# First inputs of three graph pairs in buffers of later work, weights in long runs, a re-tuned static plan, and a last layer norm by row halves

## Chip, core and metric

The kernel runs on one core of a Trainium2 chip. All times are device microseconds of one execution. A profile of one execution shows where the time goes inside it; its "span" runs from the first to the last instruction.

## What is computed

64 graphs of 256 nodes with 256 features go through two layers. Everything is in fp32.

```python
# layer 0: two graph attention steps, layer norm, feed-forward, layer norm
h = gat(x, adj, W1, a1); h = gat(h, adj, W2, a2)      # softmax(where(adj > 0, leaky_relu(e), NEG)) @ (h @ W)
h = layernorm(x + h);    h = layernorm(h + relu(h @ w_ff1 + b) @ w_ff2 + b)        # 256 -> 1024 -> 256
# layer 1: attention with 8 heads, whose weights are sorted by relation (adj == r), then the same feed-forward shape
q, k = h @ Wq, h @ Wk
out  = sum over r of (softmax(q k^T / sqrt(32)) * (adj == r)) @ (h @ Wv[r])
x = layernorm(h + out @ Wo);  out = layernorm(x + gelu(x @ W1 + b1) @ W2 + b2)
```

## The kernel before

**Tiling.** Two graphs make a pair, and 32 pairs go through `whole_way(pair)`: `gat_layers`, `feed_forward` (layer 0), `attention`, `feed_forward` (layer 1), then two stores of 256 KB. Every product is fp32 and is issued by `by_strips`, a helper at L166: four matmuls, each on 32 columns of the array. Nearly all products therefore stand under L166 in the profile, and tiles tell them apart. The products of the feed-forward and of q, k and v are done with seven block products in place of eight (the classes `Second` and `Blocks`, and `by_seven`), which needs sums of weight blocks, made once at the start (`block_sums` L446, `last_sums` L440).

**Order.** The order of instructions on every engine is fixed before the kernel runs. `run` is a list scheduler: it keeps a modelled clock per engine (`clock`, set from `START`), lets up to six pairs be under way, and asks each time which step can begin first. Steps of TensorE are chosen by a degree per kind, work of the other engines by a rank per kind. A step counts as ready when its events have happened in the model: a piece of work ends after its modelled duration plus a `lag` of 0.2 us, and TensorE prefers a step that has been ready for at least `slack` us. The table `CHANGES` resets ranks, degrees, slack and step orders at fixed model times, most of them 90 us apart, which is about one pair. `keep_order` then pins the emitted order. Each engine runs its own instructions strictly in that order, so a wait of the first one holds up all behind it.

**The first loads.** For pairs 0 and 1, `load(pair, at)` issues xT (the features, transposed), adjT (the adjacency) and x at once, and the plan is told when they land: 6.5 us and 18.0 us. For weights it is told 8, 15, 30 and 37 us. All go through the DMA queue of SP. xT of either pair goes to the one buffer `input`, so the xT of pair 1 can only be fetched once pair 0 has been read. Weights for the block products are fetched block by block: four loads of 256 KB for each of the four feed-forward matrices, eight of 64 KB for q and k, four of 128 KB for v. The later pairs are loaded by `load(pair)` with the plan's own events; their adjT and xT share `input`.

**What waits on a load.** `small_adj` (L390, ScalarE) turns adjT into bytes, `largest` (L394, VectorE) looks for empty columns. In `addends` the exponentials (L582 to L584) and a spreading over all partitions follow; in `gat_weights` VectorE makes attention weights (L630, L632) and ScalarE scales the rows (L639). L650 takes products out of the PSUM banks. L1170 and the lines near it fold biases through the weights, once.

**Layer norm.** `means` (L719) or `add_rows` gives the means of two rows-of-128, `layernorm` adds squares (L733, ScalarE), a root on GpSimd (L738, L739), and centring and scaling (L744, L747, VectorE). It works on the two row chunks of one graph. The result is turned by `transposed`: VectorE turns 32x32 blocks into `yb` (L780), SP stores them to DRAM (`home`) and gathers them back as `yT` (L785, L791); ScalarE copies `yT` into `yTa` for the attention (L973). For a few pairs at both ends (`hurried`) TensorE turns them instead (L811).

Of the kernel before, what the change touches and what calls it, by code (L numbers as in the profile page):

```python
# [10 lines left out]
F32 = mybir.dt.float32  # L11
# [7 lines left out]
P = 128  # L19
# [7 lines left out]
HURRIED = 2  # L27
SEVEN = (0, 2)
SHAPES = ("rows",)
NORMED = ()  # L30
CHANGES = (
    (27.0, ("all", "slack", 0.2), ("rank", "means", 0)),
    (117.0, ("rank", "means", 1)),
    (207.0, ("all", "qkv", ("a1", "b1", "b2", "a2", "a6", "a5", "b6", "a7", "a4", "b5", "b7", "a3", "b4", "s0", "b3", "s1")),
     ("rank", "adj", 1), ("rank", "normalise", 2), ("rank", "exp", -1)),
    (297.0, ("degree", "fill", 1), ("all", "groups", (([0], []), ([1], []), ([], [2]), ([], [3]), ([2], []), ([3], []))),
     ("degree", "first", -1), ("all", "slack", 0.3)),
    (387.0, ("degree", "fill", 2.5), ("all", "slack", 0.8), ("rank", "mask", 1.5), ("rank", "turn", 2),
     ("all", "first", ("a1", "b1", "a6", "a2", "b2", "b6", "a5", "a7", "b7", "a4", "b5", "b4", "a3"))),
    (477.0, ("all", "slack", 0.1)),  # L40
    (657.0, ("rank", "qk", 2), ("rank", "adj", 0), ("rank", "act", 0.5), ("rank", "last", 0.5)),
    (1197.0, ("rank", "invert", 1.5), ("rank", "adj", -1), ("rank", "exps", -0.5),
     ("all", "first", ("a1", "b1", "a2", "a6", "b2", "b6", "a5", "a7", "b7", "a4", "b5", "b4", "a3")),
     ("rank", "normalise", 0), ("degree", "rows", 2)),
    (1287.0, ("rank", "turn", 1)),
    (1377.0, ("all", "groups", (([0], []), ([1], []), ([], [2]), ([], [3]), ([2], []), ([3], []))), ("rank", "divide", 1.5),
     ("rank", "copies", -2), ("all", "flight", 5)),
    (1467.0, ("all", "first", ("a1", "b1", "a2", "a6", "b2", "b6", "a5", "a7", "b7", "b5", "a4", "b4", "a3")),
     ("rank", "addends", 0.5)),
    (1557.0, ("rank", "copies", 1), ("rank", "qk", -2)),  # L50
    (1827.0, ("rank", "copies", -2)),
    (1917.0, ("rank", "v", 1)),
    (2007.0, ("rank", "rows", 1.5), ("rank", "squares", -0.5), ("rank", "copies", 0)),
    (2367.0, ("rank", "last", 1), ("rank", "adj", -0.5), ("degree", "attention", 0)),
    (2547.0, ("rank", "divide", 1), ("rank", "mask", 3)),
    (2637.0, ("degree", "first", 2.5)),
    (2727.0, ("rank", "last", 3), ("rank", "second", 0.5)),
    (2817.0, ("all", "first", ("a1", "b1", "a2", "a6", "b2", "b6", "a5", "a7", "b7", "b5", "a4", "b4", "a3")),
     ("rank", "second", -0.5), ("rank", "rows", -2)),
# [6 lines left out]
        "normalise": -1, "copies": -2, "seeds": -2, "act": -1, "last": -1, "sums": -0.5, "qk": 1, "v": 1.5, "exp": 3, "mask": 0, "halves": 0, "invert": 3,  # L66
# [5 lines left out]
START = {"tensor": 8.5, "vector": 8.0, "scalar": 4.0, "gpsimd": 0.0, "sync": 32.0}  # L72
# [3 lines left out]
def two_layers(ctx: ExitStack, tc: tile.TileContext, t: dict, out: bass.AP, flag: bass.AP):  # L76
# [98 lines left out]
    nc.sync.dma_start(right[:, :, :D], t["L0_gnn_W2"].rearrange("(c p) m -> p c m", p=P))  # L175
    nc.scalar.dma_start(a2, bass.AP(tensor=t["L0_gnn_a2"].tensor, offset=t["L0_gnn_a2"].offset, ap=[[0, P], [1, 2 * D]]))
    nc.sync.dma_start(w1T, t["L0_gnn_W1T"].rearrange("(c p) m -> p c m", p=P))
# [7 lines left out]
    for columns in (slice(0, D), slice(D, D + 4)):  # L185
        for m in range(KC):
            for c in range(KC):
                by_strips(both[m][:, columns], lhsT=w1T[:, c, m * P:(m + 1) * P], rhs=right[:, c, columns],
                          start=c == 0 and columns.start == 0, stop=c == KC - 1, skip_group_check=True)
    for m in range(KC):  # L190
        nc.vector.tensor_copy(w12[:, m], both[m][:, :D + 4])
# [15 lines left out]
    free = {name: [0.0] * n for name, n in (("bank", 8 - KEPT), ("kept", KEPT), ("a", HQ), ("m", HQ), ("h", HQ), ("yb", 1), ("yT", 2), ("yTa", 1),  # L207
# [15 lines left out]
    def put(engine, us, emit, *events, rank=1, lag=0.2, kb=0, function=None, needs=None, frees=(), event=None, behind=None):  # L223
# [46 lines left out]
    def took(us):  # L270

        clock["tensor"] += us
        return at_time(clock["tensor"] + 0.2)
# [14 lines left out]
    def run(besides, ways):  # L288
# [12 lines left out]
        while True:  # L301
# [42 lines left out]
            else:  # L344
# [6 lines left out]
                clock[engine] += piece["us"]  # L351
# [10 lines left out]

    def of_graph(b):
        return slice(2 * b, 2 * b + 2)


    def load(pair, at=None):
# [4 lines left out]
        def adjT():  # L372
            if at is not None:
                to["adjT"] = work.tile([P, 2, 2, 2 * D], F32, name="v")[:, pair].bitcast(I32).rearrange(
                    "p b (c n) -> p (b c) n", c=2)
            else:
                to["adjT"] = io.tile([P, 4, N], I32, name="input")
            nc.sync.dma_start(to["adjT"], t["adjT"][rows].rearrange("b (c p) n -> p (b c) n", p=P))

        def xT():  # L380
            to["xT"] = io.tile([P, KC, 512], F32, name="input")
            nc.sync.dma_start(to["xT"], t["xT"][pair].rearrange("(c p) b n -> p c (b n)", p=P))
# [20 lines left out]
        if at is None:  # L403
# [4 lines left out]
        for emit in (xT, adjT, x):  # L408
            emit()
        return to, [at_time(at), in_bytes(at_time(at)), at_time(at)]  # L410

    def first_weights(name, wide=None):

        w = t[name]
        rows = w.shape[1] // 2
        s = const.tile([P, 7, rows], F32, name="w_" + name)
        for c, at in ((0, (0, 2)), (1, (1, 6))):
            for half, n in enumerate(at):  # L420
                nc.sync.dma_start(s[:, n], w[c * P:(c + 1) * P, half * rows:(half + 1) * rows])
        return s
# [8 lines left out]
    def last_weights(name):  # L431

        s = const.tile([P, 7, NF // 2, P], F32, name="w_" + name)
        for c, h, at in ((1, 0, 0), (0, 0, 1), (0, 1, 2), (1, 1, 3)):
            nc.sync.dma_start(s[:, at], t[name][c * FF // 2:(c + 1) * FF // 2, h * P:(h + 1) * P].rearrange("(k p) d -> p k d", p=P))
        return s

    def last_sums(w, there, event):
        for to, a, b in ((4, 3, 0), (5, 2, 4), (6, 2, 3), (3, 1, 5)):
            there = put("vector", 0.6, lambda to=to, a=a, b=b: nc.vector.tensor_tensor(w[:, to], w[:, a], w[:, b], ALU.subtract),  # L440
                        there, rank=5, event=event if to == 3 else None)
# [203 lines left out]
    def gat_layers(pair, to, loads):  # L645
        yield loads[:1], ["gat"], 2
        y = work.tile([P, 4, D + 4], F32, name="xw", bufs=2)
# [15 lines left out]
        frees_at(clock["tensor"], ["input"] * (pair > 0))  # L663
# [3 lines left out]
        for b in range(2):  # L667
            yield [e[b][1], *([] if b or not pair else [through_gat[pair - 1]])], None, 2
            if b == 0:
                z = work.tile([P, 4, D + 4], F32, name="xw", bufs=2)  # L670
# [7 lines left out]
        done_with("gat")  # L678
# [3 lines left out]
        for b in range(2):  # L682
# [7 lines left out]
            frees_at(there.time, ["e"])  # L690
            added = add_rows(to["x"], ps, b, there, loads[2])
            transposed(to["x"], layernorm(to["x"], ln[0], b, added, biased[0], stage="gat"), normal, b, pair, 0)
# [19 lines left out]
    def means(y, b, *events):  # L712
# [3 lines left out]
        def mean(j):  # L716
            if j == 0:
                of["less"] = small.tile([P, 2], F32, name="less", bufs=8)
            nc.scalar.activation(unread, y[:, 2 * b + j, :], AF.Copy, scale=-1.0 / D, accum_out=of["less"][:, j:j + 1])  # L719
# [3 lines left out]
    def layernorm(r, gb, b, added, *events, stage=None):  # L723
# [3 lines left out]
        rows = [r[:, 2 * b + j, :] for j in range(2)]  # L727
# [7 lines left out]
        def root():  # L735
# [4 lines left out]
            if stage in NORMED:  # L740
                nc.gpsimd.tensor_tensor(of["less"], of["less"], rstd, ALU.mult)
# [7 lines left out]
        def normalise(j):  # L749
            nc.scalar.activation(rows[j], rows[j], AF.Identity, bias=of["less"][:, j:j + 1], scale=rstd[:, j:j + 1])  # L750

        def onto_all(n, op):
            both = r[:, of_graph(b), :]
            nc.vector.tensor_tensor(both, both, gb[n].rearrange("p (k d) -> p k d", k=1).to_broadcast([P, 2, D]), op)

        there = put_each("scalar", 0.54, [lambda j=j: square(j) for j in range(2)], there, rank=rank_of["squares"])
        if stage in NORMED:
            there = put("gpsimd", 1.6, root, there, rank=0)
            there = put_each("scalar", 0.42, [lambda j=j: normalise(j) for j in range(2)], there, rank=rank_of["normalise"])
            return put_each("vector", 0.6, [lambda n=n, op=op: onto_all(n, op) for n, op in ((0, ALU.mult), (1, ALU.add))], there, *events,  # L760
                            rank=rank_of["scale"])
# [58 lines left out]
    def feed_forward(y, normal, w, func, relieved, gb, pair, stage):  # L820
# [44 lines left out]
        yield from (by_seven if stage in SEVEN else by_eight)(y, normal, f, evacuated, w2, w2_there, b, order)  # L865
        for g in range(2):
            normal[g] = layernorm(y, gb, g, normal["added"][g], *([biased[1]] if onwards else []), stage="ff" if onwards else "last")
# [5 lines left out]
    def by_eight(y, normal, f, evacuated, w2, w2_there, last, order):  # L873
# [790 lines left out]
```

## Time and profile before

| | us |
|---|---|
| three runs | 2926.58, 2936.07, 2936.20 (median 2936.07) |
| the profiled execution | 2928.64 |
| its span | 2926.9, so 1.74 lies around it |
| TensorE busy in the span | 2874.6 |
| VectorE, ScalarE, GpSimd busy | 2629.6, 1847.4, 274.1 |

TensorE is busy for 98% of the span. The matmuls' ends are modelled and a matmul at half clock counts as busy for twice as long, so lost time is not only in the idle 52.3 us. The distance from one matmul's start to the next is the safer measure. At full clock, 64 matmul records with 128 columns take 1.75 us from start to start (82.93 to 84.68 us in the timeline), 16 records with 256 columns 0.86 us (69.12 to 69.98 us), and 32 records with 258 columns 1.75 us. The profile splits an fp32 matmul of the program into two records.

### The profile page before, as it was taken

Reading aid. Unit: us, or ns where it says so; the run is one execution under the profiler, and the core shown is the slowest. Engines: PE = TensorE matmul, PEld = TensorE weight load, DVE = VectorE, ACT = ScalarE, POOL = GpSimd, SP = SyncE. Lnnn points to the kernel's source line nnn. Section 1 sums busy time; section 2 is a strip of 40 time slices with the busy share of each in tenths; the row PEclk is TensorE's granted clock in tenths of the full one; section 3 lists DMA queues with packets and bytes.
Section 4 is the critical chain, followed back from the end, with each engine's and each line's share of the span. In section 5 each row is a group of like instructions: output and inputs, shape, how many; then the busy total and the mean of one; then the engine's idle time right before and its main releaser. Section 6 shows DMA issues by size and latency. Waiting matters only on the chain. (4 is left out here: it accounts for less than half of the span.)

```text
span 2926.9 us, 147784 instructions
## 1 busy us (share of the span) xinstructions
PE 2874.6 (98%) x66066; PEld 2062.1 (70%) x66066; DVE 2629.6 (90%) x5874; ACT 1847.4 (63%) x5120; POOL 274.1 (9%) x518
## 2 busy tenths in 40 slices
PE   7999999999999999999999999999999999999998
PEld 4766776776776667766777767678767788677676
DVE  6899999899998889989998998999999999998887
ACT  4667666657656566565666665666666666665655
POOL 0010000100100001010100010010010000110001
PEclk8999999999999999999999999999999999999999
DMA  6222212222212222122222222221222222222100
GB/s 190 68 74 79 68 53 79 85 85 61 79 60 71 84 66 82 59 76 82 71 72 69 74 82 76 67 79 64 82 75 81 66 78 68 77 73 65 36 10 25
DMA packets 214178, 211.84 MB, mean 72 GB/s; under 512 B 22944, under 2 KB 173088, under 8 KB 213536
## 3 DMA queue, kind: packets, MB, share of 16 engines
q1 hardware_dynamic: 213120, 202.06, 22.0%
q8 instruction: 520, 8.52, 1.2%
q14 instruction: 122, 1.00, 0.1%
q10 hardware_dynamic: 416, 0.26, 0.0%
HBM read 137.51 MB, written 64.73 MB: 69 GB/s over the span
## 5 line engine op out<-in xcount | busy, mean ns | idle before, releaser
L166 PE MATMUL ps<-w_L_gnn_w_ff,ff 128*32 128x128 f32 x14336 | 426.9, 273 | 2.1 <-issue 1.4
L166 PEld LDWEIGHTS ps<-w_L_gnn_w_ff,ff 128*32 128x32 f32 x14336 | 397.3, 110 | 36.3 <-issue 13.0
L166 PE MATMUL ps<-w_L_gnn_W,ff 128*32 128x128 f32 x14336 | 418.3, 273 | 2.2 <-DVE qk L1091 0.9
L166 PEld LDWEIGHTS ps<-w_L_gnn_W,ff 128*32 128x32 f32 x14336 | 393.8, 110 | 30.6 <-issue 5.6
L1046 ACT ACTIVATE a<-ps 128x512 f32<-128x512 f32 x512 | 265.8, 600 | 145.7 <-PE ps L1037 145.0
L166 PE MATMUL ps<-yT,w_L_gnn_w_ff1p 128*32 128x256 f32 x5120 | 321.4, 382 | 10.8 <-ACT xw L650 10.6
L920 DVE TENSOR_TENSOR ff<-ff 128x1024 f32<-128x1024 f32 x256 | 311.2, 1215 | 16.0 <-PE ps L166 12.6
L738 POOL TENSOR_SCALAR rstd<-squares 128x2 f32<-128x2 f32 x256 | 78.2, 306 | 2625.1 <-ACT unread L733 2622.5
L733 ACT ACTIVATE unread<-x,less 128x256 f32<-128x256 f32 x512 | 259.6, 507 | 99.6 <-DVE less L708 68.6
L166 PE MATMUL ps<-yT,w_L_gnn_W1p 128*32 128x256 f32 x5120 | 316.0, 379 | 1.3 <-ACT ff L845 0.5
L845 ACT ACTIVATE ff<-ps 128x512 f32<-128x512 f32 x384 | 221.7, 588 | 146.5 <-PE ps L166 145.1
L1050 DVE TENSOR_TENSOR m<-a,adj 128x1024 f32<-128x1024 f32 x256 | 306.0, 1215 | 1.0 <-ACT a L1046 1.0
L517 DVE TENSOR_TENSOR ff<-ps,ff 128x512 f32<-128x512 f32 x384 | 260.2, 682 | 31.9 <-PE ps L166 20.4
L166 PE MATMUL ps<-xw,e 128*32 128x258 f32 (+1 forms) x4096 | 248.9, 385 | 5.8 <-ACT xw L639 5.8
L166 PEld LDWEIGHTS ps<-yT,w_L_gnn_w_ff1p 128*32 128x32 f32 x5120 | 172.6, 110 | 113.6 <-ACT xw L650 13.5
L166 PEld LDWEIGHTS ps<-yT,w_L_gnn_W1p 128*32 128x32 f32 x5120 | 171.9, 110 | 100.1 <-ACT ff L845 5.7
L851 ACT ACTIVATE ff<-ff,c_L_gnn_b_ff 128x256 f32<-128x256 f32 x384 | 172.8, 502 | 101.5 <-DVE ff L517 101.0
L917 DVE TENSOR_TENSOR x<-ps,x 128x256 f32<-128x256 f32 (+1 forms) x384 | 191.8, 504 | 33.8 <-PE ps L166 30.4
L166 PEld LDWEIGHTS ps<-xw,e 128*32 128x32 f32 x4096 | 138.4, 111 | 90.7 <-ACT xw L639 8.5
L739 POOL TENSOR_TENSOR rstd<-rstd,mhalf 128x2 f32<-128x2 f32 x256 | 195.2, 763 | 21.3
L851 ACT ACTIVATE ff<-ff,c_L_gnn_b 128x256 f32<-128x256 f32 x384 | 172.3, 504 | 36.8 <-DVE ff L517 35.5
L1007 ACT ACTIVATE qk<-ps,bqk 128x256 f32<-128x256 f32 x256 | 109.3, 468 | 118.3 <-PE ps L166 117.3
(133 smaller groups left out, 5091.7 us busy)
## 6 DMA issues: line engine op xcount, KB each, us to landing
home<-yb SPq DMA_DIRECT2D x182, 256.0 KB, 2.2
yT<-home SPq DMA_DIRECT2D x728, 64.0 KB, 2.1
rows<-row SPq DMA_DIRECT2D x60, 512.0 KB, 4.1
input<-in_xT SPq DMA_DIRECT2D x32, 512.0 KB, 3.8
x<-in_x SPq DMA_DIRECT2D x32, 512.0 KB, 3.9
out<-x SPq DMA_DIRECT2D x64, 256.0 KB, 2.6
input<-in_adjT SPq DMA_DIRECT2D x30, 512.0 KB, 3.9
v<-in_adjT SPq DMA_DIRECT2D x2, 512.0 KB, 7.1
```

Of the source, the lines that this page charges most:

```text
L166: nc.tensor.matmul(to[at:at + DH], lhsT=lhsT[:, at:at + DH], rhs=rhs, **flags)
L517: nc.vector.tensor_tensor(self.target(*where), self.bank["z"], self.target(*where), ALU.add)
L733: nc.scalar.activation(unread, rows[j], AF.Square, bias=of["less"][:, j:j + 1], accum_out=squares[:, j:j + 1])
L738: nc.gpsimd.tensor_scalar(rstd, squares, 1.0 / D, EPS, ALU.mult, ALU.add)
L739: nc.gpsimd.tensor_tensor(rstd, rstd, mhalf[:, :2], ALU.pow)
L845: return put("scalar", 0.5, lambda: nc.scalar.activation(target(c, h), of, AF.Copy), event, rank=rank_of["copies"])
L851: evacuated[h][m] = put("scalar", 0.4, lambda m=m, to=to, source=source: nc.scalar.activation(to, source, func, bias=b1[:, m:m + 1]), even ...
L917: return put("vector", us, lambda: nc.vector.tensor_tensor(to, of, to, ALU.add), *events, rank=rank_of["last"], frees=frees)
L920: return put("vector", 1.14, lambda: nc.vector.tensor_tensor(to, a, b, op), *events, rank=rank_of["sums"])
L1007: nc.scalar.activation(target_qk(c, b)[:, n], of[:, n], AF.Identity, bias=bqk[:, n, c:c + 1])
L1046: nc.scalar.activation(a[n][q][:, k], ps[2 * q + k], AF.Exp)
L1050: nc.vector.tensor_tensor(m[n][q], a[n][q], adj, ALU.mult)
```

## The change

It has five parts.

1. **Inputs.** `EARLY = 3`: xT of pair 0 goes to `input`, xT of pairs 1 and 2 to the two halves of the tile `qk`, adjT of all three to three of the four `m` buffers; both tiles belong to the attention, which comes later. The first product of pair 1 goes to the tile `v` in place of an `xw` buffer. The order of loads is: xT, adjT of pairs 0 and 1, x of pair 0, the first weights, xT and adjT of pair 2, further weights with x of pairs 1 and 2 among them. In setup W1T moves from SP's queue to ScalarE's, ahead of a2; the products for `w12` go half by half, and ScalarE takes out the second half.
2. **Weights in long runs.** The host lays the blocks out in the order in which they lie in the tile. A first feed-forward matrix comes in two loads (768 KB in runs of 6 KB, 256 KB in runs of 2 KB), a second one in one load of 1 MB in runs of 8 KB in place of 512 B, q with k and v in two loads each, and each layer norm's two vectors in one.
3. **Plan.** A lag of 0.3 us in place of 0.2, VectorE's durations times 1.03, new landing times (`LANDED`, `THERE`), new start clocks, the two `xw` buffers counted as a resource in place of a lock on the stage ("gat"), and a new table `CHANGES`.
4. **Last layer norm.** For the last pair the layer norm and the stores go by row halves: chunks 0 and 2 (the first half of both graphs), then 1 and 3. In the plan, the means of the first half no longer wait for the last product.
5. `NORMED`, which was empty, is removed with its branch.

On every engine the same computing instructions are issued: TensorE 33049 matmuls before and after, of the same shapes; VectorE and ScalarE differ by the one evacuation that moves; GpSimd is the same. SP issues 1217 in place of 1240. Their order differs from the start to the end.

```diff
-    (27.0, ("all", "slack", 0.2), ("rank", "means", 0)),
...
+    (27.0, ("rank", "piece", 0), ("degree", "fill", 2), ("rank", "squares", 1.5)),
...
-START = {"tensor": 8.5, "vector": 8.0, "scalar": 4.0, "gpsimd": 0.0, "sync": 32.0}
+START = {"tensor": 9.5, "vector": 9.3, "scalar": 9.7, "gpsimd": 0.0, "sync": 36.0}
+LANDED = (("ln0", 15.0), ("ff0", 18.5), ("ff0_last", 26.0), ("ln1", 28.5), ("attention", 34.5), ("ff1", 40.0), ("ff1_last", 43.0))
+THERE = ((6.5, 8.0, 13.5), (9.5, 11.0, 27.5), (20.5, 22.0, 35.0))
...
+    nc.scalar.dma_start(w1T, t["L0_gnn_W1T"].rearrange("(c p) m -> p c m", p=P))
     nc.scalar.dma_start(a2, ...)
-    nc.sync.dma_start(w1T, t["L0_gnn_W1T"].rearrange("(c p) m -> p c m", p=P))
...
-                clock[engine] += piece["us"]
+                clock[engine] += piece["us"] * (1.03 if engine == "vector" else 1.0)
...
     def last_weights(name):
         s = const.tile([P, 7, NF // 2, P], F32, name="w_" + name)
-        for c, h, at in ((1, 0, 0), (0, 0, 1), (0, 1, 2), (1, 1, 3)):
-            nc.sync.dma_start(s[:, at], t[name][...].rearrange("(k p) d -> p k d", p=P))
+        nc.sync.dma_start(s[:, :4], t[name + "m"])
...
-        yield loads[:1], ["gat"], 2
-        y = work.tile([P, 4, D + 4], F32, name="xw", bufs=2)
+        yield [loads[0], *([z_begun[pair - 1], through_gat[pair - 2]] if pair > 1 else [])], None, 2, *(["xw"] * (pair != 1))
+        y = in_values if pair == 1 else work.tile([P, 4, D + 4], F32, name="xw", bufs=2)
...
-        normal["added"] = [means(y, g, d24, d7, d3) for g in range(2)]
+        if last_of_all(pair, stage):
+            normal["added"] = [means(y, by_halves(j), d24, d7, *([d3] * j)) for j in range(2)]
+        else:
+            normal["added"] = [means(y, pair_of(g), d24, d7, d3) for g in range(2)]
...
+    of_qk = work.tile([P, 2, KC, 512], F32, name="qk")
+    homes = [work.tile([P, 2, 512], F32, name="m", bufs=HQ).rearrange("p b (c n) -> p (b c) n", c=2) for _ in range(EARLY)]
+    homes = list(zip((io.tile([P, KC, 512], F32, name="input"), of_qk[:, 0], of_qk[:, 1]), homes))
...
+    for pair in range(2):
+        emit[pair][0]()
+        emit[pair][1]()
+    emit[0][2]()
+    ln = [layernorm_weights("ln0", "L0_gnn_b_ff2")]
+    ff0 = [first_weights("L0_gnn_w_ff1p"), column("L0_gnn_b_ff1")]
+    emit[2][0]()
+    emit[2][1]()
...
+            if last_of_all(pair, 2):
+                nc.sync.dma_start(out[2 * pair:2 * pair + 2, b * P:(b + 1) * P].rearrange("g p d -> p g d"),
+                                  to["x"].rearrange("p (g j) d -> p j g d", j=2)[:, b])
...
+def by_halves(j):
+    return (j, 2 + j)
...
+def _blocks(w):
+    return w.reshape(2, P, 2, -1).transpose(1, 2, 0, 3).copy()
```

## The prediction

> **What bounds the kernel now.** I read the page's busy times first, then the windows by stage, then the timeline where TensorE has gaps, then the end. TensorE is the bound: 98% busy. The windows' columns are stretch, length, then per engine busy us and instructions, then granted clock, DMA share and GB/s.
>
> ```profile
> PE 2874.6 (98%) x66066; PEld 2062.1 (70%) x66066; DVE 2629.6 (90%) x5874; ACT 1847.4 (63%) x5120; POOL 274.1 (9%) x518
> ```
> ```profile
> 0.00:60.00 60.00, 41.44 (x529) 27.46 (x533) 33.55 (x111) 21.73 (x57) 3.18 (x10) 0.81 0.77 222
> ...
> 200.00:700.00 500.00, 499.24 (x11476) 357.15 (x11472) 462.82 (x1030) 329.17 (x906) 48.11 (x90) 1.00 0.24 74
> 700.00:1600.00 900.00, 886.58 (x20416) 622.99 (x20412) 810.78 (x1810) 565.68 (x1578) 83.31 (x156) 1.00 0.24 74
> 1600.00:2700.00 1100.00, 1097.92 (x25408) 804.56 (x25400) 1015.35 (x2276) 709.59 (x1978) 107.69 (x204) 1.00 0.23 73
> 2700.00:2880.00 180.00, 177.47 (x4096) 124.65 (x4091) 155.60 (x305) 112.82 (x300) 14.00 (x25) 1.00 0.08 27
> 2880.00:2926.90 46.90, 34.48 (x1014) 28.62 (x1006) 27.89 (x57) 21.22 (x62) 6.54 (x12) 0.91 0.08 27
> ```
>
> The matmuls are the same 33049 before and after, so the change can only move what TensorE loses: 18.6 us idle in the first 60 (and a granted clock of 0.81), 2.6 in 100 to 200, 0.8 in 200 to 700, 13.4 in 700 to 1600, 2.1 in 1600 to 2700, 2.5 in 2700 to 2880, and 12.4 at the end. The start, from the timeline (start, length, engine, line, tiles; in brackets the idle time before and who ended it):
>
> ```profile
> 10.22 1.06 ACT L390 ACTIVATE adj<-v 128x1024 uint8<-128x1024 int32 x1 [7.06 <-DMA v<-in_adjT]
> ...
> 11.05 3.71 PE L166 MATMUL ps<-w,input 128*32 128x260 f32 x64 [0.41 <-DVE w L191]
> ...
> 25.12 1.06 ACT L390 ACTIVATE adj<-v 128x1024 uint8<-128x1024 int32 x1 [7.77 <-DMA v<-in_adjT]
> ...
> 26.63 5.51 PE L166 MATMUL ps<-xw,e 128*32 128x258 f32 x64 [5.42 <-ACT xw L639]
> ...
> 42.22 1.93 PE L166 MATMUL ps<-wv,c_L_gnn_boc 128*32 128x256 f32 x16 [2.53 <-DVE wv L1159]
> ```
>
> ScalarE stood 7.77 us for the adjacency of pair 1, which the plan had for 18 us and which came at 25; the scaling of pair 0 (L639) was behind it in ScalarE's order, and TensorE behind that. Priced at full clock (64 records of 128 columns 1.75 us, 16 of 256 columns 0.86, both start to start), TensorE's rows up to 60 us are 31.9 us of work: 28.1 us are lost there. In the middle the long gaps are of one kind:
>
> ```profile
> 882.13 0.63 ACT L973 ACTIVATE yTa<-yT 128x512 f32<-128x512 f32 x1 [2.93 <-DMA yT<-home]
> ...
> 887.56 2.79 PE L166 MATMUL ps<-yT,w_L_gnn_w_ff1p 128*32 128x256 f32 x24 [3.23 <-ACT xw L650]
> ```
>
> ScalarE waits at L973 for gathered rows that the plan thought there; evacuations (L650) queue behind it, no bank is free, TensorE stops. Starts show this four times: about 3.6, 2.8, 2.1 and 3.1 us, near 884, 977, 1068 and 1248.
>
> **What the Trainium skill says.** "TensorE: Matmul & The Clock Gate", Part 1: an idle window of about 3.4 us halves TensorE's clock until it has been busy as long. The trace agrees: the matmuls after the 5.42 us wait take 5.51 us where 3.5 is the full-clock price. "DMA: Bandwidth & Descriptors", Rules for kernel authors, asks for 1 MiB or more per transfer. The trace agrees in direction: packets of 512 B took a median of 27 ns (16 engines: 303 GB/s), of 2 KB 84 ns (390 GB/s), and the whole start ran at 222 GB/s. "Perfetto Trace Analysis", Identifying the Most-Contended Engine, says that matmul busy time is no measure of distance from the peak: here 41.4 us busy hold 31.9 us of work.
>
> **The change, part by part.**
>
> *Start.* I walk the new order of TensorE, at full-clock prices, against landings estimated from bytes issued ahead. Before, 10.6 MB of first loads took until about 48 us; by 10, 20 and 30 us 2.2, 4.9 and 7.4 MB had moved. The new list is 12.2 MB with three pairs; half of the weights' short runs become long, so I take 270 to 300 GB/s from 2.3 us on.
> - Setup: W1T is issued 0.5 us sooner, a2 0.5 us later, so the four sums at L181 end near 8.8. The first feature product starts at 10.9 (11.05 before).
> - Pairs 0 and 1, 64 records each, 7.0: 17.9. Pair 1's xT has 1.8 MB ahead, lands near 11: no wait. Spreading of pair 0 (8 records, 0.9): 18.8. L1170 on the first feed-forward weights (32 records at 0.112, 3.6): these are byte 4.7 M, landing 18.5 to 20; I take 20: done 23.7. Spreading of pair 1: 24.6.
> - Product of pair 0 with its attention weights, 3.5. New wait: in ScalarE's order the byte copy of pair 2's adjacency stands ahead of L639. It is byte 5.8 M: 22 to 24 us; 1.06 for the copy and 0.9 for two scalings end at 24 to 26. TensorE: 28.1 without a wait, up to 29.5 with.
> - Pair 1, first half: its scaling waits for evacuations and for VectorE, which stands at the second layer norm's bias (planned 28.5): ready 30.2, done 32. Spreading 0.9, second half (ready 34) done 35.9. L1170 and its kin on q, k and v (3.5): 39.5. L1170 on layer 1's weights: landing 40.5, done 44.1.
> - Pair 0's second product: half at 45.9; the other half's scaling is behind the bytes of pair 3, whose load is the 37th on SP, behind all weights: 46.1, so done at 48.7. Spreading, pair 2's feature product (4.4): 53.1. TensorE's turn of pair 0's rows (1.7) meets the end of layer norm at 54.5: 55.6. The next product waits for ScalarE until 57.1.
>
> By then 39.2 us of work are done, 17.9 lost. Before, 39.2 us were done at 67.8 (31.9 by 60, then 0.6 lost), 28.6 lost. **Start: -10.7 us**; -5 if the loads come at 240 GB/s, -15 if nothing after 24 us waits. Cover: this counts as long as TensorE has no idle later for lack of pairs; before, it has none from 60 to 100. Fewer DMA issues (1217 for 1240 on SP) cost nothing by themselves; hidden behind the transfers.
>
> *Middle.* Same instructions, new order. VectorE 90% busy and TensorE 98%: the order alone decides. Against 0.17 us idle per 100 in the best stages, 700 to 1600 has 1.49: an excess of 11.9, and 3.4 for two stretches of half clock of 3.4 us after the two longest stalls. The larger lag and the 1.03 bring the model nearer to the chip (L920 is planned at 1.14, takes 1.215), but the model of the gather that causes these four stalls is left as it is. I take half of 15.3: **-8 us**; bounds -20 (100 to 200 and 2700 to 2880 gain too) and +20 (such stalls in some seven more pairs).
>
> *End.* ScalarE's eight passes run from 2914.77 at about 0.62 each, then root and L747:
>
> ```profile
> 2919.12 0.51 ACT L733 ACTIVATE unread<-x,less 128x256 f32<-128x256 f32 x1
> ...
> 2921.21 0.88 DVE L747 SCALAR_TENSOR_TENSOR x<-x,rstd,b_L_gnn_beta 128x256 f32<-128x256 f32 x2 [0.18 <-POOL rstd L739]
> ```
>
> After, the passes are two means, two squares, two means, two squares: the last square, the last root and L747 end where they did. Only the first store goes some 1.5 us earlier and leaves the queue to the second. **-0.3 us** (0 to -1). `NORMED` was empty: 0.
>
> Sum -19.0: against the profiled execution 2928.64 - 19.0 = 2909.6, span 2907.9. That execution stands 7.4 below the median of the runs, which is what is forecast: 2936.07 - 19.0 = **2917**.
>
> **Rivals.**
> 1. *Forecast*: start and half of the middle, 2917. Chance 0.52.
> 2. *All of it*: the start is gained and the stalls near 884 to 1248 go; -15 -20: 2901. For: the order is drawn with more lag. Against: the gather's model. 0.12.
> 3. *The start only*: the middle is as before, -11: 2925. 0.17.
> 4. *The wait is replaced*: in-order ScalarE stands at the byte copies of pairs 2 and 3 as it stood at pair 1's; loads at 240 GB/s put these at 26 and 51 us, TensorE idles over 3.4 us again and runs at half clock, and the later work finds nothing hidden; -4: 2932. For: the copy does stand ahead of L639. Against: TensorE has 9 us more work beside the wait. The change then does not do what it says. 0.13.
> 5. *Slower*: the new order puts L973 ahead of its gather in most pairs. Each costs about 2.9 us (mean of the four), 1.7 more where the clock halves. With the start's -11 it takes nine such pairs beyond the four to pass +14.7; in 14 more pairs: +41 -11, 2966. For: it recurred at three pairs in a row before. Against: 200 to 700 and 1600 to 2700 are nearly free of it. 0.06.
>
> **Numbers.** 0.5% is 14.7 us, about what a measurement of this kernel can tell from no change; it lies at 2921.4, and the runs before spread over 9.6. Rival 1 falls below that line in about 0.50 of its 0.52, since its own spread is what rivals 2 to 4 describe; with rival 2: faster 0.62. Rivals 3 and 4 and the rest of 1: same 0.32. Rival 5: 0.06. Range: 2899 (rival 2 and the lower standing of a run) to 2936 (rival 4).
>
> **What would show it.** Right: 45 us or more of TensorE's busy time in the first 60 at a clock over 0.85; no ScalarE wait for adjacency over 4 us after 12 us; less than 9 us idle in 700 to 1600; the same 4.8 us from the last L747 to the end. Wrong: TensorE idle for 5 us between 18 and 30 us; waits at L973 ahead of TensorE gaps in most pairs; a middle with over 30 us idle.

## The result, and the profile after

| us | before | after |
|---|---|---|
| median of 5 runs each | 2936.2 (2926.58 to 2944.82) | 2907.09 (2905.24 to 2909.98) |
| the profiled execution | 2928.64 | 2907.10 |
| its span | 2926.9 | 2905.2 |

The ratio is 0.990, with a 95% interval of 0.9878 to 0.9923: the change takes 1.0% off. The forecast was 2917 in a range of 2899 to 2936, faster as the likeliest case. Medians differ by 29.1 us and the two profiled executions by 21.5. The runs of before spread over 18 us in this comparison and those of after over 5; over all 34 runs of before in this study the median is 2933.50, 26.4 above after. The traces are compared below, so their 21.5 us are what has to be found.

The page of after, the line of busy times, and the windows by stage (stretch, length, busy us and instructions of TensorE, weight loads, VectorE, ScalarE and GpSimd, then granted clock, DMA share, GB/s):

```profile
PE 2865.5 (99%) x66066; PEld 2028.6 (70%) x66066; DVE 2634.9 (91%) x5873; ACT 1929.1 (66%) x5175; POOL 270.0 (9%) x518
```
```profile
0.00:60.00 60.00, 48.56 (x676) 31.54 (x680) 39.02 (x129) 29.81 (x81) 2.61 (x10) 0.94 0.72 240
...
200.00:700.00 500.00, 495.27 (x11358) 347.61 (x11354) 460.99 (x1030) 340.17 (x911) 43.06 (x88) 1.00 0.24 73
700.00:1600.00 900.00, 897.81 (x20742) 635.89 (x20738) 831.86 (x1855) 609.83 (x1636) 83.62 (x164) 1.00 0.24 75
1600.00:2700.00 1100.00, 1094.71 (x25372) 774.75 (x25368) 1011.52 (x2245) 737.96 (x1979) 112.14 (x200) 1.00 0.24 73
```

Three readings. In the first 60 us TensorE starts 676 matmul records in place of 529, at a clock of 0.94 in place of 0.81. In 700 to 1600 its idle time falls from 13.4 to 2.2 us. In 200 to 700 and in 1600 to 2700 it is idle *longer* than before, 4.7 for 0.8 and 5.3 for 2.1: the new order gives some of the gain back. (The trace's record of the clock begins at 9.9 us in before and at 15.5 us in after; the windows count what lies ahead of it as full.)

ScalarE is busy for 81.7 us more than before. The computing instructions are the same but for one; what grew is the number of times that it loads a function table (ACT_TABLE_LOAD in the trace), 124 in place of 70, at 1.28 us each, 69 us in all. So the new order asks more of ScalarE, which is busy for 66% of the span, and is still the faster one.

Idle time alone hides half-clock stretches, so I also counted lost time: the length of a stage, less the full-clock price (start to start) of every matmul record that starts in it. All prices together are 2826.6 us in either kernel.

| us lost in | before | after | difference |
|---|---|---|---|
| 0 to 70 | 28.7 | 19.4 | -9.3 |
| 70 to 200 | 4.7 | 3.0 | -1.7 |
| 200 to 700 | 6.9 | 10.0 | +3.1 |
| 700 to 1600 | 28.6 | 10.9 | -17.7 |
| 1600 to 2700 | 12.0 | 18.6 | +6.6 |
| 2700 to the last matmul's start | 8.0 | 5.9 | -2.1 |
| from there to the end of the span | 11.6 | 10.8 | -0.8 |

The differences add up to -21.9 by the rounded entries, -21.7 by the spans: two places carry the gain, the start and 700 to 1600.

The start, from the timeline of after (start, length, engine, line, tiles; in brackets the idle time before and who ended it):

```profile
10.02 2.31 PE L162 MATMUL ps<-xw,a 128*32 128x4 f32 x48 [3.45 <-DMA xw<-in_L_gnn_a1c]
12.15 5.36 PE L162 MATMUL ps<-w,input 128*32 128x260 f32 x64
...
22.96 1.07 ACT L393 ACTIVATE adj<-m 128x1024 uint8<-128x1024 int32 x1
...
26.86 4.80 PE L162 MATMUL ps<-xw,e 128*32 128x258 f32 x64
...
33.75 1.95 PE L162 MATMUL ps<-v,e 128*32 128x258 f32 x32 [2.08 <-ACT v L638]
...
46.10 1.06 ACT L393 ACTIVATE adj<-input 128x1024 uint8<-128x1024 int32 x1 [4.06 <-DMA input<-in_adjT]
```

The byte copy at 22.96 is pair 2's, and it has no bracket: its adjacency was there. The wait of 7.77 us for pair 1's is gone, and with it TensorE's 5.42. What waits now is the setup (3.45 us for a 2 KB load), one product for its scaling (2.08), and ScalarE for pair 3's adjacency (4.06). In the middle, the four long stalls (884, 977, 1068, 1248 us) have no successor; the longest between 100 and 2700 us is one of 1.62 at 290. The view of waits, ScalarE, 60 to 2860 us (waiting line, who ended it, us in total, times, longest), before and then after, shows the same operation under its two line numbers:

```profile
ACT yTa L973 <- DMA yT<-home: 55.8, 32, 5.7
```
```profile
ACT yTa L962 <- DMA yT<-home: 29.0, 26, 2.0
```

The end of after, timeline:

```profile
2898.25 0.51 ACT L733 ACTIVATE unread<-x,less 128x256 f32<-128x256 f32 x1
...
2900.07 0.88 DVE L745 SCALAR_TENSOR_TENSOR x<-x,rstd,b_ln 128x256 f32<-128x256 f32 x2 [0.58 <-POOL rstd L739]
```

From the last square to the last scaling it is 1.82 us, in place of 2.09, and from that scaling's end to the end of the span 4.25 in place of 4.81.

### The profile page after: what moved, and what is told of

It reads as the page before. It is cut to its first block, busy times and chain, and to the rows that moved or that the text cites. A ratio compares the mean times of both kernels' runs of the same rounds, so it can differ in the third digit from the quotient of the medians.

```text
span 2905.2 us, 147950 instructions
## 1 busy us (share of the span) xinstructions
PE 2865.5 (99%) x66066; PEld 2028.6 (70%) x66066; DVE 2634.9 (91%) x5873; ACT 1929.1 (66%) x5175; POOL 270.0 (9%) x518
## 3 DMA queue, kind: packets, MB, share of 16 engines
q1 hardware_dynamic: 206608, 201.79, 22.1%
## 4 chain that ended last, share of the span: by engine, by line
PE 86%; DVE 2%; DMA 1%; ACT 1%; issue 0%; SPq 0%; POOL 0%; DVEq 0%; POOLq 0%; ACTq 0%
PE ps L162 72%; PE ps L1057 7%; PE ps L1026 4%; PE ps L1060 2%; DMA home<-yb 1%; DMA yT<-home 0%; DVE ff L906 0%; DVE m L1039 0%; ACT unread L733 0%; DVE x L745 0%; SPq L777 0%; PE ps L797 0%; DVE x L903 0%; DVE h L1043 0%; ACT ff L831 0%
## 5 line engine op out<-in xcount | busy, mean ns | idle before, releaser
L162 PE MATMUL ps<-w_L_gnn_W,ff 128*32 128x128 f32 x14336 | 426.5, 273 | 0.5 <-DVE x L903 0.5
L162 PE MATMUL ps<-w_L_gnn_w_ff,ff 128*32 128x128 f32 x14336 | 420.5, 273 | 6.3 <-issue 4.6
L906 DVE TENSOR_TENSOR ff<-ff 128x1024 f32<-128x1024 f32 x256 | 310.8, 1214 | 16.9 <-PE ps L162 14.5
L162 PE MATMUL ps<-yT,w_L_gnn_w_ff1p 128*32 128x256 f32 x5120 | 313.5, 379 | 1.0 <-DVE qk L1080 1.0
L162 PE MATMUL ps<-yT,w_L_gnn_W1p 128*32 128x256 f32 x5120 | 306.6, 379 | 6.0 <-ACT ff L831 2.5
L831 ACT ACTIVATE ff<-ps 128x512 f32<-128x512 f32 x384 | 225.9, 593 | 126.3 <-PE ps L162 125.2
L903 DVE TENSOR_TENSOR x<-ps,x 128x256 f32<-128x256 f32 (+1 forms) x384 | 195.4, 509 | 76.6 <-PE ps L162 73.6
L162 PEld LDWEIGHTS ps<-yT,w_L_gnn_W1p 128*32 128x32 f32 x5120 | 165.1, 110 | 111.2 <-ACT ff L831 4.5
L162 PE MATMUL ps<-xw,e 128*32 128x256 f32 (+1 forms) x4032 | 239.1, 383 | 1.3 <-ACT xw L638 1.3
L162 PEld LDWEIGHTS ps<-yT,w_L_gnn_w_ff1p 128*32 128x32 f32 x5120 | 166.3, 110 | 101.0 <-DVE qk L1080 1.5
L742 DVE SCALAR_TENSOR_TENSOR x<-x,less,b_ln 128x256 f32<-128x256 f32 x512 | 226.6, 476 | 1.3 <-ACT unread L733 0.6
L745 DVE SCALAR_TENSOR_TENSOR x<-x,rstd,b_ln 128x256 f32<-128x256 f32 x512 | 222.4, 476 | 2.8 <-POOL rstd L739 2.8
```

What stands on the lines that cost most here:

```text
L162: nc.tensor.matmul(to[at:at + DH], lhsT=lhsT[:, at:at + DH], rhs=rhs, **flags)
L742: nc.vector.scalar_tensor_tensor(rows[j], rows[j], of["less"][:, j:j + 1], g, op0=ALU.add, op1=ALU.mult)
L745: nc.vector.scalar_tensor_tensor(rows[j], rows[j], rstd[:, j:j + 1], beta, op0=ALU.mult, op1=ALU.add)
L831: return put("scalar", 0.5, lambda: nc.scalar.activation(target(c, h), of, AF.Copy), event, rank=rank_of["copies"])
L906: return put("vector", 1.14, lambda: nc.vector.tensor_tensor(to, a, b, op), *events, rank=rank_of["sums"])
```

## Experiments

### The plan's parts, exchanged (e1 to e4)

The first four runs ask which part of the plan brought the middle's gain: the table `CHANGES`, or the lag of 0.3 with VectorE's 1.03.

e1, all of the plan's settings as before, on the new start:

```diff
-CHANGES = (... of after)
+CHANGES = (... of before)
-lag=0.3; clock[engine] += piece["us"] * (1.03 if engine == "vector" else 1.0)
+lag=0.2; clock[engine] += piece["us"]
```

> The changed kernel with the table CHANGES of before, a lag of 0.2 us and no factor 1.03: the new start, loads and end under the old plan's settings. Theory A (the start gives some 9 us, the middle some 11 because table and lag together were fitted to the new course of the plan): the start stays (TensorE loses about 19 us in the first 60), the middle from 100 to 2860 us loses 55 us or more again, as before; 2918 to 2930 us. Rival B (all of the gain is the start and the end, the middle would have come by itself): 2905 to 2911 us. Rival C (an old table that meets a new start is worse than either): over 2936 us.

Measured: 3035.39 us (3031.92 to 3040.70), ratio to before 1.037 (1.0337 to 1.0404).

e2, the reverse: the kernel before with the new table, the lag and the 1.03.

```diff
-CHANGES = (... of before); lag=0.2; ... piece["us"]
+CHANGES = (... of after); lag=0.3; ... piece["us"] * (1.03 if engine == "vector" else 1.0)
```

> The kernel of before with the new table CHANGES, the lag of 0.3 us and the factor 1.03, but its own first loads and landing times. Theory A: the start loses 28 us as before, and the table, fitted to another course, does not pay: middle 45 to 65 us lost, 2922 to 2936 us. Rival D (the lag and the factor make any plan good, wherever it starts): middle 40 us lost or less, about 2912 to 2918 us.

Measured: 3000.21 us (2997.36 to 3007.39), ratio 1.0248 (1.0212 to 1.0283).

e3, after with only the table of before:

```diff
-CHANGES = (... of after)
+CHANGES = (... of before)
```

> The changed kernel with only the table CHANGES of before; lag 0.3 us and factor 1.03 stay. Theory A: the middle loses 50 us or more, 2915 to 2930 us. Rival D (lag and factor do it): as the changed kernel, 2905 to 2911 us.

Measured: 3131.93 us (3124.62 to 3133.60), ratio 1.0696 (1.0663 to 1.0729).

e4, after with only the lag of before and without the 1.03:

```diff
-lag=0.3; clock[engine] += piece["us"] * (1.03 if engine == "vector" else 1.0)
+lag=0.2; clock[engine] += piece["us"]
```

> The changed kernel with a lag of 0.2 us and no factor 1.03; the new table stays. Theory A (the table fits only the course it was found for): middle 50 us lost or more, 2915 to 2930 us. Rival D: the same number, since the lag is what was taken away. Rival E (the table alone does it, lag or no lag): 2905 to 2911 us.

Measured: 3019.89 us (3017.22 to 3025.32), ratio 1.0313 (1.0279 to 1.0347).

All four are far slower than *both* kernels, by 64 us or more, and nearly all my numbers for them were too small. They do not tell which part brought the gain. What they have in common is a table that meets another course of the plan than the one it was found with, by another lag or by another start. What waits then is of many kinds. The view of waits of e3, weight loads, 60 to 2860 us:

```profile
PEld ps L168 <- issue: 94.5, 173, 14.8
PEld ps L1063 <- DVE m L1045: 48.6, 29, 4.8
...
PEld ps L168 <- DVE qk L1086: 28.5, 12, 5.5
```

The largest entry names no releaser. Among the named ones masks (L1045) and divisions (L1086) of VectorE lead; TensorE's direct waits for the gather of yT are not among the leading ones. e3 loses 284.6 us in all, and after 70 us its clock is granted at half for 126.3 us; in after it is not once before the end.

### Without any table (e10, e11)

To ask whether lag and 1.03 are a better model in themselves, the table was emptied, once with and once without them.

```diff
-CHANGES = (... of after)
+CHANGES = ()
```

> The changed kernel with an empty table CHANGES: the plan with the lag of 0.3 and VectorE's 1.03, but no settings fitted to it. Theory Q: the lag and the 1.03 make a better model of the chip in themselves, so this plan loses less than the next run's with 0.2 and 1.0: 2970 to 3020 us, and 15 us or more below the next run. Rival R: the table of settings is all, each fitted to one exact course of the plan, and two unfitted plans differ by chance: both between 3000 and 3080, within 15 us of each other or the one with 0.2 faster.

Measured: 3082.04 us (3070.31 to 3086.78), ratio 1.052 (1.0474 to 1.0565).

```diff
-CHANGES = (... of after); lag=0.3; ... piece["us"] * (1.03 if engine == "vector" else 1.0)
+CHANGES = (); lag=0.2; ... piece["us"]
```

> As the run before it (an empty table), with the lag of 0.2 and without the 1.03. Theory Q: 3000 to 3050 us, 15 us or more above the run before it. Rival R: within 15 us of it, or faster.

Measured: 3047.48 us (3043.40 to 3053.36), ratio 1.0392 (1.0345 to 1.0438).

Theory Q's forecast falls: with the larger lag and the 1.03 the unfitted plan is 35 us *slower*. Rival R holds by its second form (and 3082 is 2 us over its range). One unfitted plan of each kind doesn't show that the smaller lag is the better model; it gives the larger one no support. The new table is worth 175 us on its own plan (3082 to 2907). The view of waits, TensorE, of e10:

```profile
PE ps L139 <- DVE ff L883: 43.6, 41, 3.5
```

In 41 places TensorE waits for the sums of the feed-forward on VectorE (L906 in after, L920 before), the instruction that the prediction took as the example for the 1.03 (L883 here).

All plans beside each other, with lost time and with ScalarE's waits at the yTa copy for its gather, from 60 to 2860 us:

| | table | lag | lost to 70 | lost later | copy's waits, us (times) |
|---|---|---|---|---|---|
| before | old | 0.2 | 28.7 | 60.0 | 55.8 (32) |
| after | new | 0.3 | 19.4 | 48.4 | 29.0 (26) |
| e1 | old | 0.2 | 22.1 | 170.0 | 51.1 (27) |
| e2 | new | 0.3 | 35.3 | 125.7 | 40.4 (33) |
| e3 | old | 0.3 | 19.6 | 265.0 | 54.1 (30) |
| e4 | new | 0.2 | 22.4 | 159.0 | 35.1 (29) |
| e10 | none | 0.3 | 20.0 | 211.1 | 58.0 (40) |
| e11 | none | 0.2 | 21.7 | 192.7 | 73.6 (39) |

Two columns are worth reading down. The start's loss goes with the start (19 to 22 with the new one, under every table). And the copy's waits go with the *table*: 29 to 40 us with the new one, 51 to 74 with the old one or none, whatever the lag. The later loss doesn't follow them: e2 and e4 wait less at the copy than before and lose far more. The new table holds one entry on that copy:

```
(27.0, ("rank", "piece", 0), ...        # its rank is -2 in the old one
```

The lowest rank goes first, so under the new table the plan can put more of ScalarE's other ready work ahead of the copy, and the gather has longer to land. That this entry does it was not tried alone; the table has 45 others.

### The copy's wait alone (e9)

The kernel before, with its order kept to the instruction. Only the source of the 64 copies is changed.

```diff
             nc.scalar.activation(yT[:, b]...,
-                                 normal["yT"][:, b].rearrange("p a (ck i) -> p ck a i", i=32), AF.Copy)
+                                 ff0[0][:, 0].rearrange("p (a ck i) -> p ck a i", a=4, i=32), AF.Copy)
```

> The kernel before, with the same order on every engine; the 64 copies into yTa (L973) read the first feed-forward weights, which lie on the chip from 40 us on, in place of the gathered rows yT, so ScalarE can no longer wait for a gather there. The numbers that the attention computes with are then not the program's; the gathers themselves still run. Theory N: the copy's wait is what the four stalls near 884, 977, 1068 and 1248 us are made of, and with it what 700 to 1600 loses beyond the changed kernel (28.6 against 10.9). The loss there falls to 9 to 14, the other stages by up to 5, the time by 14 to 22 us, a ratio of 0.9925 to 0.995. Rival P: behind the copy something else is late by nearly as much (the products that bring the rows, or VectorE), so the loss in 700 to 1600 stays above 20 and the time within 8 us of before.

Measured: 2912.47 us (10 runs, 2907.30 to 2914.96) against 2932.45 (15 runs, 2920.41 to 2943.95), ratio 0.9932 (0.9914 to 0.9949): 20.0 us. The window of e9, columns as above:

```profile
700.00:1600.00 900.00, 897.72 (x20684) 637.61 (x20680) 822.84 (x1839) 575.23 (x1616) 86.10 (x162) 1.00 0.24 75
```

TensorE's idle time in 700 to 1600 is 2.3 us, as in after (2.2), and all four stalls are gone. Lost time there is 15.0 (28.6 before), one us over the upper end of theory N's 9 to 14, and the total falls from 88.7 to 71.4. Theory N holds in the main, and rival P falls: nothing else was late by nearly as much behind the copy. Nor is there a sign that the gathers ran earlier because the copy no longer reads their rows: from 60 to 2860 us SP's largest waits ahead of the store to `home` and ahead of the gather are 463.0 and 313.9 us before, 466.1 and 312.5 in e9.

The spread falls as well: the fifteen runs of before beside it span 23.5 us, the ten of e9 7.7. So most of the spread came through this wait. That the landings of the gathers vary from run to run, and that the old order passes this on, is the likely reading; no trace of a second execution shows it.

### The start's parts (e5, e6, e8, e12)

In these, the order on the computing engines is that of after; only loads are moved or cut. After was not run again beside them. e7 below, run with e5, e6 and e8, stands in for it: it has the early loads and the long runs, and 2907.53 us.

e5, weights by blocks as before:

```diff
-        nc.sync.dma_start(s[:, :3], t[name + "m"][:, :3])
-        nc.sync.dma_start(s[:, 6], t[name + "m"][:, 3])
+        for c, at in ((0, (0, 2)), (1, (1, 6))):
+            for half, n in enumerate(at):
+                nc.sync.dma_start(s[:, n], t[name][c * P:(c + 1) * P, half * rows:(half + 1) * rows])
...                                          # the second matrices, q, k and v likewise
```

> The changed kernel with the weights loaded block by block as before (four loads for each feed-forward matrix, with runs of 512 B for the second ones, eight for q and k, four for v); the two vectors of a layer norm stay in one load, and the order of all computing instructions is that of the changed kernel. Theory F (long runs bring the loads forward, and the start needs them at these times): TensorE loses 24 to 28 us up to 70 us in place of 19.4, total 2911 to 2916 us. Rival G (the early inputs alone are the gain, weights come in time either way): 2906 to 2909 us.

Measured: 2912.36 us (2910.28 to 2912.77), 5.3 over after; ratio to before 0.9915 (0.9889 to 0.9940). The first 70 us lose 25.8 for 19.4. The timeline shows where short runs come too late, at layer 1's weights:

```profile
44.47 0.72 PE L1177 MATMUL ps<-c_L_gnn_b2c,w_L_gnn_W1p 128*128 128x1 f32 x5 [0.91 <-DMA w_L_gnn_W1p<-in_L_gnn_W1p]
```

And pair 3's adjacency, behind all weights, is copied at 52.3 us in place of 46.1; there TensorE then waits 1.86 us for the scaling behind it. So long runs in few loads are worth some 5 us. The length of the runs and the number of loads change together here and were not tried apart.

e6, pair 2's loads behind the first attention weights:

```diff
-    emit[2][0]()
-    emit[2][1]()
     ff0 += [last_weights("L0_gnn_w_ff2"), Event()]
...
-    emit[2][2]()
+    for each in emit[2]:
+        each()
```

> The changed kernel with the loads of pair 2 (xT, adjT, x) put behind the first weights of the attention, where its x stood; all computing instructions keep their order. ScalarE's byte copy of pair 2's adjacency then waits for about 9 MB, to about 32 us, in place of 23. Theory H (each engine's fixed order hands that wait to TensorE): some 8 us more idle between 24 and 33 us and 1 to 2 us of half clock, 2915 to 2919 us. Rival I (other pairs' work covers it): under 2910 us.

Measured: 2916.08 us (2913.16 to 2916.78), 9.0 over after; ratio 0.9926 (0.9901 to 0.9952). The timeline:

```profile
33.77 1.06 ACT L393 ACTIVATE adj<-m 128x1024 uint8<-128x1024 int32 x1 [11.33 <-DMA m<-in_adjT]
...
35.28 6.53 PE L162 MATMUL ps<-xw,e 128*32 128x258 f32 x64 [7.98 <-ACT xw L638]
```

This is before's wait again, one pair later: the byte copy stands ahead of pair 0's scaling (L638), and TensorE behind that, 7.98 us, and then at half clock (6.53 for 3.5 us of work; the trace has half clock from 24.0 to 41.1). The first 70 us lose 30.6, more than before's 28.7. So an order that takes pair 2 early must also *load* it early: in this order the early place in the queue is worth 9 us. That is as much as the start gains in all, but it is not the sum of the start's parts: e5 takes 5.3 us of the same gain away by another part, and no run moves pair 1's inputs back.

e8, the 2 KB load that the setup waits for, put first on ScalarE's queue:

```diff
+    nc.scalar.dma_start(right[:, :, D + 2:], t["L0_gnn_a1c"])
     nc.scalar.dma_start(w1T, ...)
     nc.scalar.dma_start(a2, ...)
-    nc.scalar.dma_start(right[:, :, D + 2:], t["L0_gnn_a1c"])
```

> The changed kernel with the 2 KB load of a1c issued first on ScalarE's queue, ahead of W1T and a2, in place of last. In the changed kernel TensorE stands 3.45 us for it in setup, until 10.02 us. Theory J (that wait opens the whole start later): setup is over about 0.6 us sooner (then the sums on VectorE, done at 9.47, are the last), less half clock, 1 to 2 us gained, 2905 to 2906 us. Rival K (later waits of the start are for landings at fixed times and take it back): the first feature product starts sooner, but by 70 us the same 19.4 us are lost; no change of the total.

Measured: 2908.36 us (2906.66 to 2910.11), as after. The wait for that load went, and another took its place: W1T comes at 6.53 us in place of 4.64, TensorE then waits for the sums on VectorE, and the first feature product starts *later*. So neither theory was put to its test, which asked for an earlier start. The timeline of e8:

```profile
10.88 0.28 PE L162 MATMUL ps<-xw,a 128*32 128x4 f32 x8 [2.41 <-DVE h L177]
...
13.39 4.50 PE L162 MATMUL ps<-w,input 128*32 128x260 f32 x64
```

e12, 1 MB of weights moved behind pair 3's adjacency:

```diff
-    ff1 = [..., last_weights("L1_gnn_W2"), Event()]          # this is issued ahead of load(3)
+    if pair == EARLY: nc.sync.dma_start(ff1[2][:, :4], ...)   # in load's adjT, behind it
```

> The changed kernel, same order on every computing engine; on SP's queue the 1 MB of layer 1's second feed-forward weights is issued behind the adjacency of pair 3 in place of ahead of it. In the changed kernel ScalarE waits 4.06 us for that adjacency at 46.1 us. Theory S: the byte copy of pair 3 starts 3 us or more sooner (43 or less), the first 70 us lose 1 to 3 us less than 19.4, and the time falls by 1 to 3 us, 2904 to 2906. Rival T: the copy starts sooner but TensorE's next wait, for layer norm's rows near 57 us, is set by VectorE and not by this copy: the loss and the time stay within 1 us.

Measured: 2907.00 us (2903.47 to 2908.56), as after, and 19.6 lost to 70 us. The copy no longer waits, by the timeline of e12:

```profile
42.00 1.04 ACT L395 ACTIVATE adj<-input 128x1024 uint8<-128x1024 int32 x1
```

Rival T's forecast holds: 4.06 us of ScalarE's idle time were worth nothing, for TensorE was not behind them. In after its 64 records at 45.92 us did not wait, and its next wait, near 57 us, stays (1.41 lost there for 1.52).

### The end (e7)

```diff
     def last_of_all(pair, stage):
-        return (pair, stage) == (NPAIR - 1, 2)
+        return False
```

> The changed kernel with the last layer norm and stores by graph as before, nothing else. By the prediction's step the end gives 0.3 us; by the two profiles, from the first of the last four means to the end of the span, 12.1 us before and 11.1 after, so 1.0. Expected here: 0.3 to 1.0 us more, in the end alone; total 2907 to 2909 us. A rival: nothing at all, the 1.0 being another execution's chance.

Measured: 2907.53 us (2906.76 to 2909.99), against 2907.09: not to be told apart. In the profiles, from the first of the last four means to the end of the span it is 11.8 us in e7, 11.1 in after, 12.1 before. The timeline of e7:

```profile
2899.73 0.88 DVE L745 SCALAR_TENSOR_TENSOR x<-x,rstd,b_ln 128x256 f32<-128x256 f32 x2 [0.18 <-POOL rstd L739]
```

The first mean is at 2893.31 there, so 6.42 us pass to this scaling, 6.00 in after. Halves are worth 0.7 us in single profiles, at most that, and nothing in the medians.

No run beat after by more than the runs' spread.

## Why the prediction came out as it did

**The bound and the two places**: right. TensorE's loss was to fall in the start and in 700 to 1600, and nowhere else does it fall by more than 2.1 us.

**"Start: -10.7 us"**: measured -9.3. Its mechanism, a byte copy in ScalarE's order that holds up the scaling and TensorE behind it, is shown by e6 for pair 2; for pair 1 it is read from the two traces. Its two bad steps lie inside the sum:

- *Setup*, "the first feature product starts at 10.9": it started at 12.15. I counted W1T and a2 on ScalarE's queue and left out the load behind them, a1c, which W1T pushed to third place: issued at 1.79 us, it landed near 10. That product then ran at half pace: four records every 0.43 us until 15.57 us and every 0.22 us from there, where before's took 0.22 nearly from its start. So the next product began at 17.32, some 2.9 us later than I had it. In e8 the first product starts 1.24 us later still, but its slow part ends at 15.09, the next one begins only 0.40 later, and the loss to 70 us is 19.5 for 19.4. Whether an earlier start would gain was not tried.
- The walk used full-clock prices and left out what the clock does to them. Beside that slow beginning, two stretches of 3.4 us ran at half clock, 25.8 to 29.2 and 46.3 to 49.7: 1.7 us of work lost in each. The windows of after (granted clock third from the right) show them and what stood ahead of them:

```profile
21.80:25.40 3.60, 3.60 (x36) 3.60 (x34) 3.15 (x11) 2.43 (x8) 0.00 (x0) 1.00 1.05 368
25.80:29.20 3.40, 3.40 (x30) 1.91 (x32) 3.30 (x9) 2.64 (x8) 0.00 (x0) 0.50 0.73 247
42.20:45.90 3.70, 3.70 (x36) 3.64 (x32) 1.69 (x8) 0.00 (x0) 0.00 (x0) 1.00 0.58 194
46.30:49.70 3.40, 3.40 (x40) 1.74 (x32) 2.56 (x6) 1.66 (x3) 0.00 (x0) 0.51 0.34 73
```

TensorE was not idle ahead of them: it was busy with the bias folding, 32 matmul records of *one column* each.

The prediction's own example of half clock needs the same care. It set the 5.51 us of the product at 26.63 in before's trace down to the wait of 5.42 us ahead of it. The clock there fell at 20.14 us, inside the block of one-column records that ends at 21.22, before the wait began; so that example does not show an idle window at work. The stalls of the middle do: behind those near 884 and 1248 us, with 3.23 and 2.73 us idle, half clock follows for 3.4 us each time, and behind those near 977 and 1068 us, with 2.44 and 1.80 us idle, it does not.

Against this the transfers ran better than the 270 to 300 GB/s that I took. The view of DMA of after, 12 to 34 us, has

```profile
DMA packets 5191, 7.13 MB, mean 324 GB/s; under 512 B 1118, under 2 KB 3871, under 8 KB 5061
```

so no product waited for weights, where I had put waits to 20 and 40.5 us. (The times of packets of 512 B and 2 KB, which I set beside a rule on the size of a transfer, speak of the length of a run and not of that size.) The pair 3 byte copy was forecast for 46.1 and came at 46.10, but the idle of about 1.1 us that I hung on it (45.9 to 48.7, less 1.75 of work) didn't come: TensorE reached that product at 45.92, at half clock, and did not stand. The errors nearly cancel: the walk's end, the product forecast for 57.1 us, came at 58.95.

**"Middle: I take half of 15.3: -8 us"**: the mis-sized term. From 70 us to the last matmul it was -11.8. In 700 to 1600 alone it was -17.7, more than all of the 15.3, and e9 confirms that the 15.3 was a fair size for the stalls (13.6 there, and 20.0 in the median). I halved it because "the model of the gather that causes these four stalls is left as it is". That was true of the model and wrong as a reason: the wait also depends on where the copy stands in ScalarE's order, and over the eight plans side by side the copy's waits go with the table and not with the lag. The other half of the reason, that lag and 1.03 bring the model nearer to the chip, found no support in e10 and e11. And I had no term for what a new order gives back: +3.1 in 200 to 700 and +6.6 in 1600 to 2700, in waits under 2 us of many kinds, whose causes I did not separate.

**"End: -0.3 us" (0 to -1)**: inside its bounds; the profiles have -0.8. "The last square, the last root and L747 end where they did" was not quite so: from the first of the last four means to the last scaling it is 6.00 us for 6.44. By e7 the halves give 0.7 at most.

**"All of it"**, which I gave 0.12, told the middle better than the forecast: the start was gained, and all four stalls went. Its 2901 had no term for the loss that came back elsewhere; the measured 2907.09 lies 6 us from it and 10 from my 2917. **"The start only" and "The wait is replaced"** fell, the first by the middle, the second by the byte copy at 22.96. **"Slower"** described the right mechanism with the wrong sign: L973 ahead of its gather was what the old order suffered from, and the new one has less of it (29.0 us for 55.8).

**The sum**: -19.0 for -21.5 in the profiled executions. That it came so near is in part luck: in the middle 17.7 us gained at one place and 9.7 given back at two others, neither of them forecast at that size, left something near my -8. The other 7.6 us of the medians' 29.1 are no step of mine: before's profiled execution stood 7.4 under its median, and I carried that over to after, whose profiled execution stands on its median (2907.10 for 2907.09). e9 shows that the waits which made before slow also carried most of its spread.

**What would show it**: 48.56 us busy at 0.94 (45 at 0.85 asked), no wait for adjacency over 4 us after 12 us but for pair 3's 4.06, 2.2 idle in 700 to 1600 (under 9), 4.25 from the last scaling to the end (the same 4.8 was asked; each of the last four stores is 256 KB in both kernels, and why this stretch is shorter was not found out).

## What to carry to other kernels

In a plan fixed ahead of time, look for an in-order engine that stands in front of a transfer the model thinks landed: the wait is short, but all that queues behind it is not, and here taking that one wait away was worth 20.0 us. Giving such a copy a later turn is a way to try; it was not tried alone here. Treat such a plan's settings as one fitted whole: change one modelled constant and fit again, for a part taken over alone cost 64 us or more here in all four combinations tried. When a trace shows a long idle on an engine off the critical path, ask who stands behind it before you remove it (7.77 us of ScalarE's at one place held up TensorE for 5.42, and 4.06 at another cost nothing).

## What the runs showed of the hardware

**Blocks of one-column matmuls stood ahead of half clock.** "TensorE: Matmul & The Clock Gate", Part 1, in the Trainium skill, speaks of an idle window of about 3.4 us. That says nothing of products of one column. Here a block of 32 one-column records, 3.6 to 3.7 us long without idle time inside, is followed at once by half clock: in after 21.87 to 25.50 and half clock from 25.8, 42.26 to 45.99 and half clock from 46.3; in before 50.47 to 54.10 and half clock from 54.3. TensorE did not wait just ahead of any of the three. Each of the 14 traces has two such blocks, some with short waits inside, and in 27 of the 28 cases half clock begins inside the block or at most 1.2 us after its end. The exception is the second block of e8, 44.02 to 47.76 us: the product behind it runs at full pace. So such a block does not bring half clock every time. That the blocks are the cause is argued from this sequence; no run spread them among wide products.

**A small load is not early because it is small.** a1c has 2 KB. Third on ScalarE's queue it landed 8.1 us after its issue (after), behind two loads of 256 KB that took 3.9 and 6.3. Second it took 6.0 (before), first 3.1 (e8). Its place on the queue went with its time; what else was on the way at that moment was not held fixed.
